# Four slots in thirteen summed, and 0.5 carried from the second layer's relu: a four-layer graph network on one core

## The chip, the cores and the metric

The kernel runs on one core of one Trainium2 chip. The metric is the device time of one launch in microseconds (us). Three runs of the kernel before gave 4869.19, 4869.73 and 4886.89 us; the median is 4869.73 us. All figures about where time goes come from one further, profiled execution, whose own time was 4870.96 us.

## The reference

The input is `x` with 64 graphs of 256 nodes and 128 features, and one 256 x 256 adjacency `adj`. Four layers follow each other, each of the form `h = relu(layernorm(x)); x = x + layer(h)`:

```
layer 0: five steps of a gated recurrent unit, fed by adj @ h
layer 1: relu([h, A h, (2 A A - 1) h, ...] @ Theta1 + bias)
layer 2: y = (adj @ h + h) @ weight + bias;  y / max(|y|, 1e-12)
layer 3: pre[i,j,:] = s1[i,:] + s2[j,:] + b_lin
         e[i,j] = sum_e a[e] * leaky_relu(pre[i,j,e]) + adj[i,j]
         sigmoid(softmax_j(e) @ h)
```

Layer 3 is the large one: for every graph, 256 x 256 pairs of nodes with 256 features each. The kernel computes the final sigmoid as `0.5 + 0.5 * tanh(...)`, and that 0.5 is one subject of the change. A layernorm subtracts the mean of a row, so a constant added to the whole row leaves what it returns as it was.

## The kernel before, in words

The graphs go in 32 pairs (`NPAIR`), two graphs at a time. For each pair a long chain of small steps, `front` (L484 on), computes layers 0 to 2 and the projections that layer 3 needs. The scores of layer 3 are then built in *slots*: 64 per pair, 2048 in all. A slot stands for four nodes of one 128-node half, one out of each group of 32, in both graphs, against all nodes and features. The features come in two halves of 128, and each half of a slot is a *tile* of 128 x 2048 float32 values: an elementwise minimum or relu of one projected value per partition against a row of the other projection. So there are 4096 tiles. `work_on_tile` (L910) makes them on whichever of three engines takes them: VectorE makes one with one instruction (L930), ScalarE with eight activations of 128 x 256 (L942), and GpSimd with eight tensor-scalar instructions of 128 x 256 (L947). Fourteen buffers (`rl`) hold tiles. TensorE reduces a tile over its partitions into a bank of PSUM with four matmuls of 32 columns (`score`, L1006), each recorded as two passes in float32.

In some slots the two halves are summed first, so that TensorE has one tile to reduce and not two. `JOINED` lists those slots from the constant `SHARE`: of the first 1952 slots (the last `ALONE` = 96 are left out) one in three, that is 650. For a joined slot, the sum is made by a DMA that GpSimd issues and that adds one buffer onto another (`add_pair`, L967). The buffer added from comes free when this DMA has landed; the other, when TensorE has read it.

The order of the work is made while the program is written. A planner keeps a clock per engine and hands out steps by modelled durations: `ran(DVE, 2.2, ...)` for a VectorE tile, 1.43 for half a ScalarE tile, 0.9 for a quarter of a GpSimd tile, `ISSUE` = 0.65 for the issue of a DMA, `LANDED` = 6.6 until it has landed, and named constants (`TURN`, `STATS` and others, L456 to L458) for the steps of a front. The engine whose clock stands lowest takes, of what is ready then, a step of a tail first, then of a front, and a tile only when no such step is ready. `in_order` then fixes that order: on the chip, each engine runs its own list strictly in that sequence and waits where something it needs is late. A changed modelled duration therefore changes no instruction, but it moves instructions in the lists and decides which engine makes which tile.

When the tiles of 32 slots have been reduced, `tail` (L805) finishes them on two banks' worth of rows: VectorE adds the odd feature's term (L812, two instructions from PSUM into PSUM) and the linear row (L816, from PSUM into SBUF), takes the row maximum (L821), ScalarE does the exponential (L825), TensorE turns and multiplies, ScalarE takes tanh (L849, two instructions), and VectorE makes `o = 0.5 * tanh + x3` (L853), which a DMA from SP's queue stores. The 0.5 of the sigmoid is in `x3` by then: GpSimd adds it in place (L713), once per pair, after the last layernorm has read `x3`.

Of the kernel before, what the change touches and what calls it, by code (L numbers as in the profile page):

```python
# [10 lines left out]
OP = mybir.AluOpType  # L11
# [3 lines left out]
P = 128  # L15
NB = 2
# [5 lines left out]
MOST_POSITIVE = -MOST_NEGATIVE  # L22
PE, DVE, ACT, POOL = ENGINES = (mybir.EngineType.PE, mybir.EngineType.DVE, mybir.EngineType.Activation, mybir.EngineType.Pool)
SLOTS = 64
SHARE = (1, 3)
AHEAD_OF = 2
ALONE = 96
LOW = 1
# [4 lines left out]
def kernel(  # L33
# [50 lines left out]
    nc = tc.nc  # L84
    B, N, D = x.shape
# [21 lines left out]
    def ran(engine, us, *after):  # L107
        start = max(clock[engine], 0.0, *after)
        if engine == ACT:
            behind[0] = max(0.0, behind[0] - (start - clock[ACT])) + 0.024 * us  # L110
        clock[engine] = start + us
        return clock[engine] + SEEN[engine] + (behind[0] if engine == ACT else 0.0)
# [13 lines left out]
    def by_feature(b, nb=NB):  # L126
        return b[:, 0:nb * N].rearrange("p (b n) -> p b n", b=nb)
# [64 lines left out]
    bias1 = load_row(l1_bias, "bias1")  # L192
# [71 lines left out]
    def other_constants():  # L264
# [5 lines left out]
        t = ran(DVE, 0.8)  # L270

        for c in range(NC):
            yield PE, t, 1
            b = take()
            for k in range(NC):
                nc.tensor.matmul(b[0][:, 0:N], adj_t[:, k, c * P:(c + 1) * P], adj_n[:, k, :], start=(k == 0), stop=(k == NC - 1))
            t = ran(PE, 1.2, t, b[1])
            yield DVE, t
            nc.vector.tensor_scalar(adj_2[:, c, :], b[0][:, 0:N], 2.0, None, op0=OP.mult)
            t = ran(DVE, 0.35, t)  # L280
# [1 line left out]
        yield DVE, 12.0  # L282
        nc.vector.tensor_add(th[:, 1:3, :], th_raw[:, 1:3, :], th_raw[:, 3:5, :])
        nc.vector.tensor_sub(th[:, 0, :], th_raw[:, 0, :], th[:, 2, :])
        ran(DVE, 0.5)
        yield DVE, clock[DVE]
        small = work.tile([P, 32], F32, name="small", bufs=1)

# [14 lines left out]
        t = ran(DVE, 1.5)  # L303
        yield PE, t, 1
        b = take()
# [5 lines left out]
        t = ran(PE, 0.6, t, b[1])  # L311
        yield DVE, t
        nc.vector.tensor_copy(columns(14, 3), b[0][:, 0:3])
        t = ran(DVE, 0.1, t)
# [27 lines left out]
        t = ran(DVE, 1.6)  # L342
# [11 lines left out]
        for c in range(NC):  # L354
            yield PE, t, 1
            b = take()
# [3 lines left out]
            t = ran(PE, 1.2, t, b[1])  # L360
# [5 lines left out]
            t = ran(DVE, 0.35, t)  # L366
# [3 lines left out]
        b = take()  # L370
# [8 lines left out]
        t = ran(PE, 1.4, t_in, b[1])  # L379
# [9 lines left out]
        t = ran(DVE, 0.9, t)  # L389
# [54 lines left out]
    def feat(name, **kw):  # L444
        return work.tile([P, NB, N], F32, name=name, **kw)
# [7 lines left out]
    SHORT = dict(tag="short", bufs=12)  # L453


    PROJECT, MIX, TURN, PRODUCT, PRODUCTS = (None, 0.44, 0.86), (None, 0.88, 1.74), (None, 0.55, 0.80), (None, 0.45, 0.88), (None, 1.33, 2.64)  # L456
    COPY, BIASED, TANH, ELEMENTS = (None, 0.32, 0.48), (None, 0.40, 0.58), (None, 0.40, 0.57), (None, 0.36, 0.61)
    NORMED, STATS, LAST = (None, 0.78, 1.55), (None, 0.40, 0.8), (None, 0.55, 1.04)  # L458

    def norm(src, since, h):  # L460

        nb = src.shape[1]
        stats = work.tile([P, nb * NC, 3], F32, name="stats", bufs=4)
        mv = work.tile([P, nb * NC, 2], F32, name="mv", bufs=4)
        s, h = rows_of(src), rows_of(h)[:, :, 0:D]
        yield DVE, since
        for k in range(0, nb * NC, 2):
            nc.vector.bn_stats(stats[:, k:k + 2, :].rearrange("p k s -> p (k s)"), s[:, k:k + 2, :].rearrange("p k d -> p d k"))
        nc.vector.tensor_reduce(mv[:, :, 0], stats[:, :, 1:2], AX.X, OP.add, negate=True)
        t = ran(DVE, STATS[nb], since) + 0.1  # L470
        yield POOL, t
        inverse_root(mv[:, :, 1], stats[:, :, 2], 1.0 / D, OP.mult, LN_EPS, OP.add)
        nc.gpsimd.tensor_mul(mv[:, :, 0], mv[:, :, 0], mv[:, :, 1])  # L473
        t = ran(POOL, 1.55, t)
        yield ACT, t
        for k in range(nb * NC):
            nc.scalar.activation(h[:, k, :], s[:, k, :], AF.Relu, bias=mv[:, k, 0:1], scale=mv[:, k, 1:2])  # L477
        return ran(ACT, NORMED[nb], t)
# [5 lines left out]
    def front(p, batches):  # L484
# [5 lines left out]
        alone = nb < NB  # L490
# [28 lines left out]
        def turned_of(b):  # L519
            return by_token(b[0], nb)  # L520
# [11 lines left out]
        t = yield from norm(x0, 20.0 if p else 3.0, h)  # L532
        yield PE, t, 1
        b = take()
        to_feature(b[0], h)
        t_h = t
        t = ran(PE, TURN[nb], t, b[1])
        yield ACT, t
        hT, t_hT = copied("hT", b, t, bufs=4)
        for step in range(STEPS):  # L540
            yield PE, t_h, 1, lambda: "adj" in SET_UP
            b = take()
            mix_nodes(b[0], h, adj_t)
            t = ran(PE, MIX[nb], t_h, b[1])
            yield ACT, t
            mT, t_m = copied("mT", b, t)
            if alone:
# [6 lines left out]
                t = ran(PE, PROJECT[nb], t_m)  # L554
# [6 lines left out]
            else:  # L561
# [4 lines left out]
                t = ran(PE, 2 * PROJECT[nb], t_m, t_hT, pr[1])  # L566
# [3 lines left out]
            t = ran(ACT, TANH[nb], t, r[1])  # L570
# [5 lines left out]
            if alone:  # L576
# [5 lines left out]
                t = ran(PE, PROJECT[nb], t_rh)  # L582
            else:
# [6 lines left out]
                t = ran(PE, 2 * PROJECT[nb], t_rh, pv[1])  # L590
# [6 lines left out]
            if alone:  # L597
                nc.scalar.activation(seen(pv), seen(pv), AF.Tanh, bias=bh, scale=1.0)
                t = ran(ACT, TANH[nb], t)
                yield DVE, t  # L600
                nc.vector.tensor_sub(d, seen(pv), hT)
                t = ran(DVE, ELEMENTS[nb], t)
                spare.append([pv[0], t])
            else:
                nc.scalar.activation(seen(pv), seen(pv), AF.Tanh, bias=bh_n, scale=-1.0)
                t = ran(ACT, TANH[nb], t)
                yield DVE, t
                nc.vector.tensor_add(d, seen(pv), hT)  # L608
                t = ran(DVE, ELEMENTS[nb], t)
# [3 lines left out]
            t = ran(DVE, ELEMENTS[nb], t, t_z)  # L613
# [7 lines left out]
            b = take()  # L621
            to_token(b[0], hT)
            t = ran(PE, TURN[nb], t_hT, b[1])
# [7 lines left out]
        x1 = token("x1", tag="x12", bufs=3)  # L631
        nc.vector.tensor_add(x1, x0, turned_of(b))
        t = ran(DVE, ELEMENTS[nb], t)
# [6 lines left out]
        b = take()  # L640
        mix_nodes(b[0], h, adj_n)
        t = ran(PE, MIX[nb], t_h, b[1])
# [3 lines left out]
        b = take()  # L646
        to_feature(b[0], h)
        t = ran(PE, TURN[nb], t_h, b[1])
        yield ACT, t
        hT, t = copied("hT", b, t, bufs=4)  # L650
        yield PE, t_h, 1
        b = take()
        mix_nodes(b[0], h, adj_2)
        t = ran(PE, MIX[nb], t_h, b[1])
        yield ACT, t
        c2T, t = copied("c2T", b, t)
        yield PE, t, 1
        po = take()
        project_token(po[0], [(hT, th[:, 0, :]), (c1T, th[:, 1, :]), (c2T, th[:, 2, :])])
        t = ran(PE, PRODUCTS[nb], t, po[1])  # L660
# [3 lines left out]
        t = ran(DVE, ELEMENTS[nb], t)  # L664
        yield DVE, t
        x2 = token("x2", tag="x12", bufs=3)
        nc.vector.scalar_tensor_tensor(x2, turned_of(po), 0.0, x1, op0=OP.max, op1=OP.add)
        t = ran(DVE, ELEMENTS[nb])
        spare.append([po[0], t])

# [2 lines left out]
        t = yield from norm(x2, t, h)  # L673
        yield PE, t, 1
        b = take()
        mix_nodes(b[0], h, adj_ti)
        t = ran(PE, MIX[nb], t, b[1])
        yield ACT, t
        yT, t = copied("yT", b, t)
        yield PE, t, 1  # L680
        po = take()
        project_token(po[0], [(yT, w2)])
        t = ran(PE, PRODUCT[nb], t, po[1])
# [3 lines left out]
        t = ran(DVE, ELEMENTS[nb], t)  # L687
# [21 lines left out]
        h3 = kept("h3", [NC, D + 1])  # L709
        nc.gpsimd.memset(h3[:, :, :, D:D + 1], 2.0)  # L710
        t = yield from norm(x3, t, h3)
        yield POOL, t
        nc.gpsimd.tensor_scalar(x3, x3, 0.5, None, op0=OP.add)  # L713
        ran(POOL, 0.45 if alone else 0.7, t)
        yield PE, t, 1
        b = take()
        to_feature(b[0], h3)
# [87 lines left out]
    def tail(u, pe, since):  # L805

        ops = READY[u]
        x3, h3, pe, lin = ops["x3"], ops["h3"], [by_feature(pe[0])[:, k, :] for k in range(NB)], ops["lin"]
        yield DVE, max(since, ops["t_lin"])
        sc = feat("sc", **SHORT)  # L810
        for k, (b, c) in enumerate(across(u)):
            nc.vector.scalar_tensor_tensor(pe[k], ops["s2o"][:, b, :], ops["s1o"][:, b, c:c + 1], pe[k], op0=OP.min, op1=OP.add)  # L812
        t = ran(DVE, 0.8, since, ops["t_lin"])
        yield DVE, t
        used = banks_of.pop(u)
        nc.vector.tensor_add(sc, by_feature(used), lin.to_broadcast([P, NB, N]) if ops["alone"] else lin)  # L816
        t = ran(DVE, ELEMENTS[2], t)
        spare.append([used, t])
        yield DVE, t
        nmx = work.tile([P, NB], F32, name="nmx")  # L820
        nc.vector.tensor_reduce(nmx, sc, AX.X, OP.max, negate=True)  # L821
        t = ran(DVE, ELEMENTS[2], t)
        yield ACT, t
        for b in range(NB):
            nc.scalar.activation(sc[:, b, :], sc[:, b, :], AF.Exp, bias=nmx[:, b:b + 1], scale=1.0)  # L825
        t_s = ran(ACT, 0.8, t)
        yield PE, t_s, 1
        b = take()
        to_token(b[0], sc)
        t = ran(PE, TURN[2], t_s, b[1])  # L830
        yield ACT, t
        wT = tok("wT", **SHORT)
        nc.scalar.copy(wT, by_token(b[0]))
        t = ran(ACT, COPY[2], t)
        spare.append([b[0], t])
        yield PE, t, 1
        bank = take()
        po = bank[0][:, :NB * (D + 1)].rearrange("p (b d) -> p b d", b=NB)
        for k, (b, _) in enumerate(across(u)):
            for c in range(NC):  # L840
                side_by_side(po[:, k, :], wT[:, k, c, :], h3[:, b, c, :], c == 0, c == NC - 1)
        t = ran(PE, PRODUCT[2], t, bank[1])
        yield DVE, t
        rs = work.tile([P, NB], F32, name="rs")
        nc.vector.reciprocal(rs, po[:, :, D])
        t = t_s = ran(DVE, 0.15, t)
        yield ACT, t
        for k in range(NB):
            nc.scalar.activation(po[:, k, 0:D], po[:, k, 0:D], AF.Tanh, scale=rs[:, k:k + 1])  # L849
        t = ran(ACT, 0.5, t, t_s)  # L850
        yield DVE, t
        o = work.tile([P, NB, D], F32, name="o")
        nc.vector.scalar_tensor_tensor(o, po[:, :, 0:D], 0.5, x3[:, 0] if ops["alone"] else x3[:, :, u[1], :], op0=OP.mult, op1=OP.add)  # L853
        t = ran(DVE, 0.36, t)
        spare.append([bank[0], t])
        p, k = u
        nc.sync.dma_start(out[p * NB + k].rearrange("(c p) d -> p c d", p=P) if ops["alone"] else
                          out[p * NB:(p + 1) * NB, k * P:(k + 1) * P, :].rearrange("b p d -> p b d"), o)
        TAILED.add(u)
# [269 lines left out]
```

## Time and profile before

| | |
|---|---|
| median of three runs | 4869.73 us |
| profiled execution, its own time | 4870.96 us |
| span of the profile | 4869.2 us |
| TensorE busy (records) | 4729.6 us |
| VectorE busy | 4666.6 us |
| ScalarE busy | 4630.5 us |
| GpSimd busy | 4693.2 us |
| share of time that the 16 DMA engines spent on the summing queue | 69.9% |
| mean granted TensorE clock | 0.997 |

The profile lists busy time by engine, then groups of equal instructions with their count, the busy time of the group (time in which at least one of its records was open), the mean length of one record, and the idle time of the engine directly ahead of them with what ended it. Records of matmuls and activations overlap, so a mean length times a count is more than the busy time; what one instruction takes of its engine is better read as the distance between starts in a dense stretch of the timeline. "PE" is TensorE, "DVE" VectorE, "ACT" ScalarE, "POOL" GpSimd. A line such as L967 is the line of the kernel that issued the instruction.

### The profile page before, as it was taken

How to read it: one execution, taken by the hardware profiler on the slowest of the kernel's cores; microseconds unless marked ns; L12 is line 12 of the kernel's file. 1: busy time of each engine (PE TensorE's matmuls, PEld its weight loads, DVE VectorE, ACT ScalarE, POOL GpSimd, SP SyncE). 2: the span in 40 equal slices, each digit the busy share in tenths (PEclk: the TensorE clock that was granted, in tenths of full speed). 3: DMA queues.
4: the chain of work that ended last, by engine and by line, in shares of the span. 5: the costliest groups of instructions: out<-in, count | busy, mean ns of one | idle time of the engine just before them, and what ended most of it. 6: DMA issues, size and time to landing. Idle time of an engine off the chain costs nothing.

```text
span 4869.2 us, 134117 instructions
## 1 busy us (share of the span) xinstructions
PE 4729.6 (97%) x52183; PEld 1750.1 (36%) x52183; DVE 4666.6 (96%) x3571; ACT 4630.5 (95%) x12119; POOL 4693.2 (96%) x9914
## 2 busy tenths in 40 slices
PE   9999999999999999999999999999999999999999
PEld 4333333333333333333333333333333333333333
DVE  6999999999999999999999999999999999999998
ACT  6999999999999999999999999999999999999999
POOL 3999999999999999999999999999999999999998
PEclk9999999999999999999999999999999999999999
DMA  1778777777777787777877777877777777787830
GB/s 46 158 148 165 159 155 160 158 153 163 156 158 156 149 165 160 153 162 152 165 160 155 160 153 156 166 156 155 163 147 162 161 160 157 154 163 155 165 65 5
DMA packets 138729, 725.21 MB, mean 149 GB/s; under 512 B 15721, under 2 KB 50921, under 8 KB 54889
## 3 DMA queue, kind: packets, MB, share of 16 engines
q0 software_dynamic: 93600, 681.62, 69.9%
q1 hardware_dynamic: 43768, 35.01, 2.5%
q8 instruction: 408, 6.68, 0.5%
q14 instruction: 233, 1.90, 0.1%
q10 hardware_dynamic: 720, 0.00, 0.0%
HBM read 26.48 MB, written 8.52 MB: 7 GB/s over the span
## 4 chain that ended last, share of the span: by engine, by line
PE 48%; POOL 16%; DVE 15%; DMA 10%; ACT 6%; issue 4%; POOLq 0%; DVEq 0%; SPq 0%; ACTq 0%
PE bank L1006 29%; PE bank L402 17%; POOL rl L947 13%; DVE rl L930 12%; DMA rl<-rl 10%; ACT rl L942 4%; POOL rl L967 1%; PE bank L433 1%; PE bank L425 1%; POOL mv L397 1%; DVE hT L616 1%; DVE bank L612 0%; ACT h L477 0%; DVE d L608 0%; DVE rh L573 0%
## 5 line engine op out<-in xcount | busy, mean ns | idle before, releaser
L930 DVE TENSOR_TENSOR rl<-s1a,bank 128x2048 f32<-128x2048 f32 x1751 | 3921.6, 2279 | 105.7 <-DMA rl<-rl 75.4
L942 ACT ACTIVATE rl<-bank,s1b 128x256 f32<-128x256 f32 x10032 | 3946.2, 691 | 75.4 <-DMA rl<-rl 48.1
L947 POOL TENSOR_SCALAR rl<-s2n,s1b 128x256 f32<-128x256 f32 x6352 | 3043.6, 789 | 28.4 <-DMA rl<-rl 8.6
L1006 PE MATMUL bank<-rl,win_n 128*32 128x512 f32 x17536 | 2209.3, 594 | 49.0 <-DMA rl<-rl 46.3
L1006 PE MATMUL bank<-rl,win 128*32 128x512 f32 x10032 | 1331.7, 594 | 0.0
L947 POOL TENSOR_SCALAR rl<-s2c,s1a 128x256 f32<-128x256 f32 x2376 | 1155.4, 747 | 5.0 <-DMA rl<-rl 0.7
L1006 PEld LDWEIGHTS bank<-rl,win_n 128*32 128x32 f32 x17536 | 568.9, 110 | 1195.5 <-issue 929.9
L967 POOL DMA_DIRECT2D rl<-rl x650 | 689.4, 1077 | 9.4 <-PE bank L1006 2.2
L1006 PEld LDWEIGHTS bank<-rl,win 128*32 128x32 f32 x10032 | 330.3, 110 | 637.1 <-issue 525.3
L402 PE MATMUL bank<-mT,wts 128*32 128x512 f32 x2480 | 324.9, 592 | 0.2 <-ACT mT L525 0.2
L402 PE MATMUL bank<-adj_t,h 128*32 128x256 f32 x4960 | 299.0, 380 | 7.8 <-ACT h L627 7.6
L402 PEld LDWEIGHTS bank<-adj_t,h 128*32 128x32 f32 x4960 | 160.3, 110 | 170.0 <-issue 42.8
L477 ACT ACTIVATE h<-x,mv 128x128 f32<-128x128 f32 x376 | 162.7, 572 | 41.3 <-POOL mv L473 41.2
L402 PE MATMUL bank<-rh,u5t 128*32 128x512 f32 x1240 | 162.1, 593 | 8.0 <-DVE rh L573 7.9
L402 PE MATMUL bank<-hT,wts 128*32 128x512 f32 x1240 | 164.1, 596 | 0.0
L402 PE MATMUL bank<-mT,w 128*32 128x512 f32 x1240 | 162.4, 593 | 0.4 <-ACT bank L569 0.4
L569 ACT ACTIVATE bank<-bank,gate_b 128x512 f32<-128x512 f32 (+1 forms) x165 | 138.5, 840 | 20.9 <-PE bank L402 13.6
L402 PEld LDWEIGHTS bank<-mT,wts 128*32 128x32 f32 x2480 | 81.6, 110 | 186.0 <-issue 149.6
L397 POOL TENSOR_TENSOR mv<-mv,minus_half 128x4 f32<-128x4 f32 (+1 forms) x132 | 134.0, 1015 | 11.0
L525 ACT COPY mT<-bank 128x512 f32<-128x512 f32 x155 | 119.5, 771 | 26.2 <-PE bank L402 26.0
L592 ACT ACTIVATE bank<-bank,gate_b 128x512 f32<-128x512 f32 (+1 forms) x165 | 134.1, 813 | 10.2 <-PE bank L402 9.9
L433 PE MATMUL bank<-ident,hT 128*128 128x128 f32 x620 | 101.5, 286 | 38.1 <-DVE hT L616 37.8
(206 smaller groups left out, 3354.9 us busy)
## 6 DMA issues: line engine op xcount, KB each, us to landing
rl<-rl POOLq DMA_DIRECT2D x650, 1024.0 KB, 8.4
rows<-row SPq DMA_DIRECT2D x31, 512.0 KB
xin<-in_x_dram SPq DMA_DIRECT2D x64, 128.0 KB
out_dram<-o SPq DMA_DIRECT2D x64, 128.0 KB
row<-quarter SPq DMA_DIRECT2D x62, 2.0 KB
rows<-row SPq DMA_DIRECT2D x2, 256.0 KB
w_raw<-in_L_gnn_w_w_dram SPq DMA_DIRECT2D x3, 128.0 KB
rl<-in_L_gnn_Theta_dram SPq DMA_DIRECT2D x1, 320.0 KB
```

The lines of the kernel that those rows point to most:

```text
L397: nc.gpsimd.tensor_tensor(t, t, minus_half[:, 0:t.shape[1]], op=OP.pow)
L402: nc.tensor.matmul(o[g:g + 32], w[:, g:g + 32], t, start=start, stop=stop, skip_group_check=True)
L433: nc.tensor.transpose(pt[:, b, c, :], ht[:, b, c * P:(c + 1) * P], ident)
L477: nc.scalar.activation(h[:, k, :], s[:, k, :], AF.Relu, bias=mv[:, k, 0:1], scale=mv[:, k, 1:2])
L525: nc.scalar.copy(c, seen(bank))
L569: nc.scalar.activation(seen(r), seen(pr), AF.Tanh, bias=br, scale=0.5)
L592: nc.scalar.activation(seen(pr), seen(pr), AF.Tanh, bias=bz, scale=0.5)
L930: nc.vector.tensor_tensor(t, rows.to_broadcast(whole), ops["s2a"].unsqueeze(1).to_broadcast(whole), op=OP.min)
L942: nc.scalar.activation(t[:, g, b, :], other(ops["s2p"][0], b), AF.Relu, bias=rows[:, g, b], scale=-1.0)
L947: nc.gpsimd.tensor_scalar(t[:, part, b, :], other(ops["s2n" if k else "s2c"], b), rows[:, part, b], MOST_NEGATIVE, op0=OP.min, op1=OP.max)
L967: nc.gpsimd.dma_start(out=t.rearrange("p g b n -> p (g b n)"), in_=z.rearrange("p g b n -> p (g b n)"), accum_op=OP.add)
L1006: nc.tensor.matmul(pe[g * 32:(g + 1) * 32, :], w[:, 31 - r:63 - r], flat(t[:, g]), start=False, stop=(left[u] == 0), skip_group_check=True)
```

## The change

The final 0.5 is no longer added to `x3`. Layer 1's output is `x2 = x1 + relu(p + bias)`. The layernorms of layers 2 and 3 take the constant out again, and `x3` inherits it. The GpSimd instruction of each pair is deleted.

In the tail, the linear row is added first, in place in PSUM, and the odd feature's term second, from PSUM into SBUF: the same three VectorE instructions with other destinations.

`SHARE` goes from one slot in three to four in thirteen: 600 joined slots, not 650. Five modelled durations of the planner change: `TURN` from 0.55 and 0.80 to 0.38 and 0.60, `STATS` from 0.40 and 0.80 to 0.50 and 0.87, the GpSimd part of a norm from 1.55 to 1.69, and the tanh of a tail from 0.5 to 0.9. They are no instructions, but the planner lays out every list anew with them.

```
-SHARE = (1, 3)
+SHARE = (4, 13)
...
+        nc.vector.tensor_scalar(bias1, bias1, 0.5, None, op0=OP.add)
+        ran(DVE, 0.7)
...
-    ..., TURN, ... = ..., (None, 0.55, 0.80), ...
+    ..., TURN, ... = ..., (None, 0.38, 0.60), ...
-    NORMED, STATS, LAST = (None, 0.78, 1.55), (None, 0.40, 0.8), (None, 0.55, 1.04)
+    NORMED, STATS, LAST = (None, 0.78, 1.55), (None, 0.50, 0.87), (None, 0.55, 1.04)
...
-        t = ran(POOL, 1.55, t)
+        t = ran(POOL, 1.69, t)
...
-        nc.vector.scalar_tensor_tensor(x2, turned_of(po), 0.0, x1, op0=OP.max, op1=OP.add)
+        nc.vector.scalar_tensor_tensor(x2, turned_of(po), 0.5, x1, op0=OP.max, op1=OP.add)
...
-        yield POOL, t
-        nc.gpsimd.tensor_scalar(x3, x3, 0.5, None, op0=OP.add)
-        ran(POOL, 0.45 if alone else 0.7, t)
...
+        used = banks_of.pop(u)
+        nc.vector.tensor_add(by_feature(used), by_feature(used), lin.to_broadcast([P, NB, N]) if ops["alone"] else lin)
+        t = ran(DVE, ELEMENTS[2], since, ops["t_lin"])
+        yield DVE, t
         sc = feat("sc", **SHORT)
         for k, (b, c) in enumerate(across(u)):
-            nc.vector.scalar_tensor_tensor(pe[k], ops["s2o"][:, b, :], ops["s1o"][:, b, c:c + 1], pe[k], op0=OP.min, op1=OP.add)
+            nc.vector.scalar_tensor_tensor(sc[:, k, :], ops["s2o"][:, b, :], ops["s1o"][:, b, c:c + 1], pe[k], op0=OP.min, op1=OP.add)
-        t = ran(DVE, 0.8, since, ops["t_lin"])
-        yield DVE, t
-        used = banks_of.pop(u)
-        nc.vector.tensor_add(sc, by_feature(used), lin.to_broadcast([P, NB, N]) if ops["alone"] else lin)
-        t = ran(DVE, ELEMENTS[2], t)
+        t = ran(DVE, 0.8, t)
...
-        t = ran(ACT, 0.5, t, t_s)
+        t = ran(ACT, 0.9, t, t_s)
```

More of the change, by code (lines that the diff above doesn't have):

```diff
@@ L284, in other_constants @@
         nc.vector.tensor_sub(th[:, 0, :], th_raw[:, 0, :], th[:, 2, :])
-        ran(DVE, 0.5)
+        nc.vector.tensor_scalar(bias1, bias1, 0.5, None, op0=OP.add)
+        ran(DVE, 0.7)
         yield DVE, clock[DVE]
@@ L453 @@
     SHORT = dict(tag="short", bufs=12)
-    PROJECT, MIX, TURN, PRODUCT, PRODUCTS = (None, 0.44, 0.86), (None, 0.88, 1.74), (None, 0.55, 0.80), (None, 0.45, 0.88), (None, 1.33, 2.64)
+    PROJECT, MIX, TURN, PRODUCT, PRODUCTS = (None, 0.44, 0.86), (None, 0.88, 1.74), (None, 0.38, 0.60), (None, 0.45, 0.88), (None, 1.33, 2.64)
     COPY, BIASED, TANH, ELEMENTS = (None, 0.32, 0.48), (None, 0.40, 0.58), (None, 0.40, 0.57), (None, 0.36, 0.61)
-    NORMED, STATS, LAST = (None, 0.78, 1.55), (None, 0.40, 0.8), (None, 0.55, 1.04)
+    NORMED, STATS, LAST = (None, 0.78, 1.55), (None, 0.50, 0.87), (None, 0.55, 1.04)
     def norm(src, since, h):
```

## The prediction

> **What bounds the kernel now.** I read the page's busy line first, then the groups, the chain that ended last, the waits, and the timeline for real distances between starts.
>
> ```profile
> span 4869.2 us, 134117 instructions
> PE 4729.6 (97%) x52183; PEld 1750.1 (36%) x52183; DVE 4666.6 (96%) x3571; ACT 4630.5 (95%) x12119; POOL 4693.2 (96%) x9914
> PE 48%; POOL 16%; DVE 15%; DMA 10%; ACT 6%; issue 4%; POOLq 0%; DVEq 0%; SPq 0%; ACTq 0%
> ```
>
> Four engines are within 2% of each other, and the chain (third line) runs over all of them, with summing DMAs as a tenth of it. No engine alone sets the end. The stretches say when:
>
> ```profile
> 0.00:92.00 92.00, 83.61 (x1185) 44.62 (x1189) 46.97 (x145) 46.46 (x109) 14.81 (x43) 1.00 0.10 28
> 92.00:4740.00 4648.00, 4524.94 (x49901) 1656.59 (x49905) 4504.26 (x3363) 4465.53 (x11689) 4567.36 (x9625) 1.00 0.76 155
> 4740.00:4850.00 110.00, 110.00 (x1012) 44.22 (x1012) 108.83 (x58) 109.39 (x303) 110.00 (x246) 1.00 0.02 4
> ```
>
> The columns after the length are busy PE, PEld, DVE, ACT, POOL, then clock, DMA share and GB/s. The first 92 us are set-up and the first front, which the change barely touches. From there to 4740 us POOL is busy 98.3%, DVE 96.9%, ACT 96.1%. PE's 97.4% is too high: in the timeline
>
> ```profile
> 1000.58 1.04 PE L1006 MATMUL bank<-rl,win 128*32 128x512 f32 x8
> 1001.44 1.90 PE L1006 MATMUL bank<-rl,win_n 128*32 128x512 f32 x16
> 1003.15 1.04 PE L1006 MATMUL bank<-rl,win 128*32 128x512 f32 x8
> ```
>
> a tile's eight records are open for 1.04 us but the next tile starts 0.86 us later, so every run of matmuls hides up to 0.18 us of possible waiting. Counting by such distances (3446 tiles x 0.86 = 2964; a front 5 x (one mix 1.73 + five projections of 0.86 + one turn 0.58) = 33 and about 14 for its layers 1 to 3, so 47 x 32 = 1504; 64 tails at 2.35 = 150) PE works about 4620 us, some 95% of the span. POOL works nearest its limit; PE has more air than its busy line says.
>
> ```profile
> L947 POOL TENSOR_SCALAR rl<-s2n,s1b 128x256 f32<-128x256 f32 x6352 | 3043.6, 789 | 28.4 <-DMA rl<-rl 8.6 <-ACT s1b L782 5.1 <-DVE x L667 1.8
> L967 POOL DMA_DIRECT2D rl<-rl x650 | 689.4, 1077 | 9.4 <-PE bank L1006 2.2 <-issue 2.2 <-POOL rl L947 2.1
> L713 POOL TENSOR_SCALAR x<-x 128x512 f32<-128x512 f32 (+1 forms) x33 | 48.4, 1468 | 3.8 <-ACT h L477 1.3
> L812 DVE SCALAR_TENSOR_TENSOR bank<-rows,s1o,bank 128x256 f32<-128x256 f32 x128 | 62.4, 487 | 16.8 <-PE bank L1006 14.1 <-issue 0.3
> L816 DVE TENSOR_TENSOR sc<-bank,rows 128x512 f32<-128x512 f32 x64 | 43.7, 682 | 0.0
> ```
>
> These are the groups that the change touches. The waits on the summing DMA:
>
> ```profile
> DVE rl L930 <- DMA rl<-rl: 75.4, 60, 3.8
> ACT rl L942 <- DMA rl<-rl: 48.1, 28, 4.4
> PE bank L1006 <- DMA rl<-rl: 46.3, 41, 2.8
> ```
>
> DVE and ACT wait for a buffer that a DMA still reads, PE for a sum not yet landed: 170 us over three engines, the largest waits that cross engines in the joined stretch.
>
> **What the skill says.** The Trainium skill, "Perfetto Trace Analysis", Identifying the Most-Contended Engine: matmul busy time is no fair measure of TensorE's headroom, while occupancy is for the others. The trace agrees (1.04 us open against 0.86 us apart). "DMA: Bandwidth & Descriptors", SWDGE vs HWDGE vs iDMA: accumulating DMAs must be issued by GpSimd, whose cores compute the descriptors, so a join costs POOL time; the trace agrees (row L967). "VectorE: DVE Perf Modes", The perf-mode tier table: a float32 operand in PSUM holds `tensor_tensor` to one element a cycle. The trace agrees: L816 into SBUF takes 682 ns, and L663, the same operation into PSUM, 694 ns.
>
> **The change part by part.** Counts come from the instruction lists of the two built programs.
>
> *Joins.* 50 DMA issues go. A record lasts 1.08 us, but in the timeline an issue at 2421.69 is followed by the next GpSimd tile at 2422.32, so it takes 0.63 us: 50 x 0.63 = 31.5 us off POOL. In return PE reduces 3496 tiles, not 3446: 50 x 0.86 = 43 us onto PE.
>
> *The 0.5.* L713 is deleted: 48.4 us off POOL (1.51 us each; in the timeline the next tile starts 1.58 us after it). Nobody waits for it, so its worth is POOL's time alone. The constant in L667 costs nothing more; the one `bias1` instruction lies in the set-up, below 0.3 us by L816's size. It adds a wait for the load of `bias1`, with the first fronts' VectorE steps behind it; that load follows `theta`'s on SP's queue, for which the two instructions ahead of it wait anyway, so 0 to 2 us, and I take 0.
>
> *Tiles.* POOL gets 11 tiles more (1102), ACT 7 fewer (1247), DVE 4 fewer (1747). A POOL tile takes 3.60 us (2418.14 to the next work at 2421.69): +39.6. A DVE tile takes 2.24 (3921.6 / 1751): -9.0. An ACT tile takes 2.97 (16 activations in 5.93 us are two tiles): -20.8.
>
> *The tail's order.* The add goes PSUM to PSUM (694 ns in L663's row against 682), the odd term PSUM to SBUF; L616 against L612 is the same pair of destinations, 679 against 692. Per tail 0.69 + 2 x 0.48 against 0.97 + 0.68: within 0.02 us, 1 us in all. The length to the maximum, and when the bank comes free, are unchanged; both orders wait for the same row DMA. SP's list has 243 instructions in both; no transfer but the 50 joins goes.
>
> *The modelled durations.* No instruction, but new lists. By the trace, the old ones had L713 at 0.7 (is 1.5: 31 x 0.8 = 25 us that the plan did not know of on POOL), the tail's tanh at 0.5 (two records of 0.51 in a row, 64 x 0.4 = 26 us on ACT), and a turn at 0.80 (four transposes take 0.6: 312 x 0.2 = 62 us that PE didn't need). The new list's lateness against its plan should be less. It can't be read off the trace; I bound it by -15 and +15 us and take -4, a tenth of ACT's 48.5 us of waiting for a norm's POOL part.
>
> *Sum by engine:* POOL -31.5 - 48.4 + 39.6 = -40; ACT -21; DVE -9; PE +43.
>
> POOL, DVE and ACT draw on one stock of tiles. Weighted by their shares of the chain (16, 15, 6): (16 x 40 + 15 x 9 + 6 x 21) / 37 = 24 us shorter. Their waits for the DMA are 133 us with POOL's 9.3, or 44 each. One join in thirteen fewer takes 3 us of it by count; the queue, busy 69.9%, clears faster, so up to a fifth (9 us): I take 7. PE's 43 us must come out of some 240 us in which it is not working, about 90 of which are at the two ends: at 4840 us it would work about 97% of the middle. I take 5 us lost on the way, where a bank or buffer is released later; the ends are 0 (all in the gaps) and 43.
>
> Sum: -24 - 7 + 5 - 4 = -30 us against the profiled 4871 us (span 4869.2 and 1.8 around it), which is 1.2 us above the median: about 4840 us.
>
> **Rivals.**
>
> *It cancels.* Take the chain's shares at face value for all four. PE holds 48%, so its 43 us cost 0.48 x 43 = 21. POOL gives 0.16 x 40 = 6.4, DVE 1.4, ACT 1.3. The chain's DMA share is 502 us; 50 of 650 fewer would be 39, but a route only a few us shorter takes the place of each, so a fifth, 8, stays. Net +4: about 4874 us. For it: the long PE pieces in the chain. Against it: PE is fed by the three others, and a PE piece on the chain may be one that merely ran while they would have been next.
>
> *TensorE becomes the bound, slower.* In 4740 to 4850 us, where nothing is joined, PE is busy without a gap: fewer joins move the middle towards that. PE's waits on the front (38 us for turned hidden states, about 35 for other steps) don't shrink, and if POOL's relief only fills buffers sooner, the whole 43 us less some 9 of DMA waiting is added: 4903 us; half-way, 4887. It decides once PE's real share in the middle goes over about 98%; I reckon 97%. Against it: POOL is at 98.3% with PE at 95 to 96%.
>
> *The re-made plan is much better*, beyond 15 us: less lateness on all engines, 4790 us. Nothing in the profile prices it.
>
> That the change doesn't do what it says is excluded by the lists: 600 joins, no L713.
>
> **How the numbers follow.** First case (relief of the elementwise engines) 0.62, own range 4815 to 4862; cancels 0.20; PE the bound 0.15; better plan 0.03. 0.5% is 24 us, about what a measurement of this kernel can tell from no change: below 4845 is faster, above 4894 slower. The first case gives 0.44 faster and 0.18 same; the second 0.02, 0.15 and 0.03; the third 0.03 same and 0.12 slower; the last 0.03 faster. Together 0.49, 0.36, 0.15. The range 4805 to 4892 holds the first case with the bounds of the plan's lateness, the second, and half-way to the third.
>
> **What would show it.** Right: 600 issues at L967; POOL's busy time down by about 40 us, PE's records up by about 45; the DVE and ACT waits for DMA down from 75 and 48; POOL's share of the chain down and PE's up. A PE busy over 98.5% with longer DVE and ACT waits on L1006 (13.8 and 19.5 us now) would show the slower rival. Wrong also if the DMA waits grow in spite of fewer joins, which only the new order could do.

## The result, and the profile after

The kernel after takes 4796.69 us (median of four runs, 4794.88 to 4801.95) against 4869.47 us for the kernel before measured with it. (One of the four runs of before took 4886.89 us; the other three lie within 0.6 us of each other.) The ratio is 0.984, with a 95% interval of 0.982 to 0.987: 73 us, or about 1.5%, faster. The forecast was 4840 us, with a range from 4805 to 4892, and faster at a chance of 0.49. So the sign was right, the forecast gain of 30 us was less than half of what came, and the time lies below the range.

The head of the profile of the kernel after: span, busy time by engine, and the chain that ended last.

```profile
span 4794.6 us, 134766 instructions
PE 4744.3 (99%) x52583; PEld 1758.2 (37%) x52583; DVE 4651.6 (97%) x3568; ACT 4608.6 (96%) x12063; POOL 4636.5 (97%) x9919
PE 69%; DVE 10%; POOL 8%; DMA 6%; ACT 5%; issue 2%; POOLq 0%; SPq 0%; DVEq 0%; ACTq 0%
```

PE now has a record open during all but 50 us of the span (140 before), and it holds 69% of the chain (48% before). Three engines have less work and one has more. The span is down by 75 us, and busy time by 15 us on DVE, 22 on ACT and 57 on POOL. For DVE and ACT the larger part of the 75 us is therefore waiting that is gone; for POOL it is work. Two rows of before, whose idle time matters:

```profile
L930 DVE TENSOR_TENSOR rl<-s1a,bank 128x2048 f32<-128x2048 f32 x1751 | 3921.6, 2279 | 105.7 <-DMA rl<-rl 75.4
L942 ACT ACTIVATE rl<-bank,s1b 128x256 f32<-128x256 f32 x10032 | 3946.2, 691 | 75.4 <-DMA rl<-rl 48.1
```

The same two after, with the groups that the prediction named:

```profile
L940 ACT ACTIVATE rl<-bank,s1b 128x256 f32<-128x256 f32 x9976 | 3937.4, 704 | 47.5 <-DMA rl<-rl 18.7
L928 DVE TENSOR_TENSOR rl<-s1a,bank 128x2048 f32<-128x2048 f32 x1747 | 3909.3, 2276 | 41.4 <-DMA rl<-rl 19.5
L945 POOL TENSOR_SCALAR rl<-s2n,s1b 128x256 f32<-128x256 f32 x6408 | 3056.0, 799 | 19.5 <-ACT s1b L780 5.1
L1004 PE MATMUL bank<-rl,win_n 128*32 128x512 f32 x17992 | 2241.6, 593 | 20.8 <-DMA rl<-rl 14.9
L965 POOL DMA_DIRECT2D rl<-rl x600 | 644.9, 1090 | 3.6 <-PE bank L1004 0.9
```

(L928, L940, L945, L965, L1004 are L930, L942, L947, L967 and L1006 of before.) 600 issues stand where 650 stood, L713 is gone, and the waits for the summing DMA are 19.5 us on DVE, 18.7 on ACT and 14.9 on PE, where they were 75.4, 48.1 and 46.3. Idle time ahead of DVE's tiles fell from 105.7 to 41.4 us. Yet a sum took hardly less time to land. These are the issues of the sums, before and after, and their last number is the median time in us from issue to landing:

```profile
rl<-rl POOLq DMA_DIRECT2D x650, 1024.0 KB, 8.4
rl<-rl POOLq DMA_DIRECT2D x600, 1024.0 KB, 8.3
```

In the stretch from 92 to 4665 us, PE has a record open 99.3% of the time (97.4% in the middle before), and POOL is busy 98.7%:

```profile
92.00:4665.00 4573.00, 4539.28 (x50276) 1669.61 (x50272) 4488.19 (x3355) 4444.16 (x11635) 4514.78 (x9638) 1.00 0.72 146
```

### The profile page after: what moved, and what is told of

Read it like the earlier page. It is cut to its first block, busy times and chain, and to the rows that moved or that the text cites. A ratio compares the mean times of both kernels' runs of the same rounds, so it can differ in the third digit from the quotient of the medians.

```text
span 4794.6 us, 134766 instructions
## 1 busy us (share of the span) xinstructions
PE 4744.3 (99%) x52583; PEld 1758.2 (37%) x52583; DVE 4651.6 (97%) x3568; ACT 4608.6 (96%) x12063; POOL 4636.5 (97%) x9919
## 4 chain that ended last, share of the span: by engine, by line
PE 69%; DVE 10%; POOL 8%; DMA 6%; ACT 5%; issue 2%; POOLq 0%; SPq 0%; DVEq 0%; ACTq 0%
PE bank L1004 43%; PE bank L403 23%; DVE rl L928 8%; POOL rl L945 7%; DMA rl<-rl 5%; ACT rl L940 3%; PE bank L434 2%; PE bank L426 1%; POOL rl L965 1%; ACT h L478 0%; DVE bank L613 0%; DVE d L609 0%; DVE hT L617 0%; DVE rh L574 0%; POOL mv L398 0%
## 5 line engine op out<-in xcount | busy, mean ns | idle before, releaser
L940 ACT ACTIVATE rl<-bank,s1b 128x256 f32<-128x256 f32 x9976 | 3937.4, 704 | 47.5 <-DMA rl<-rl 18.7
L928 DVE TENSOR_TENSOR rl<-s1a,bank 128x2048 f32<-128x2048 f32 x1747 | 3909.3, 2276 | 41.4 <-DMA rl<-rl 19.5
L945 POOL TENSOR_SCALAR rl<-s2n,s1b 128x256 f32<-128x256 f32 x6408 | 3056.0, 799 | 19.5 <-ACT s1b L780 5.1
L1004 PE MATMUL bank<-rl,win_n 128*32 128x512 f32 x17992 | 2241.6, 593 | 20.8 <-DMA rl<-rl 14.9
L1004 PE MATMUL bank<-rl,win 128*32 128x512 f32 x9976 | 1317.3, 593 | 0.0
L945 POOL TENSOR_SCALAR rl<-s2c,s1a 128x256 f32<-128x256 f32 x2408 | 1167.1, 763 | 3.5
L1004 PEld LDWEIGHTS bank<-rl,win_n 128*32 128x32 f32 x17992 | 577.4, 110 | 1197.8 <-issue 978.2
L965 POOL DMA_DIRECT2D rl<-rl x600 | 644.9, 1090 | 3.6 <-PE bank L1004 0.9
L1004 PEld LDWEIGHTS bank<-rl,win 128*32 128x32 f32 x9976 | 324.8, 110 | 636.4 <-issue 516.5
L606 ACT ACTIVATE bank<-bank,gate_b 128x512 f32<-128x512 f32 x155 | 128.8, 831 | 6.3 <-PE bank L403 6.3
```

The costliest lines, as they stand in the source:

```text
L928: nc.vector.tensor_tensor(t, rows.to_broadcast(whole), ops["s2a"].unsqueeze(1).to_broadcast(whole), op=OP.min)
L940: nc.scalar.activation(t[:, g, b, :], other(ops["s2p"][0], b), AF.Relu, bias=rows[:, g, b], scale=-1.0)
L945: nc.gpsimd.tensor_scalar(t[:, part, b, :], other(ops["s2n" if k else "s2c"], b), rows[:, part, b], MOST_NEGATIVE, op0=OP.min, op1=OP.max)
L965: nc.gpsimd.dma_start(out=t.rearrange("p g b n -> p (g b n)"), in_=z.rearrange("p g b n -> p (g b n)"), accum_op=OP.add)
L1004: nc.tensor.matmul(pe[g * 32:(g + 1) * 32, :], w[:, 31 - r:63 - r], flat(t[:, g]), start=False, stop=(left[u] == 0), skip_group_check=True)
```

## The experiments

The change has four parts: the *share* (600 joins), the *modelled durations* (four steps, not five: the turn, the statistics, the norm's GpSimd part and the tanh), *L713* deleted, and the *tail's order*. The expectations weigh five theories of where the 73 us come from:

- L: fewer joins alone clear the DMA queue.
- P: the corrected durations make the planned order fit the chip.
- W: it is the work taken off GpSimd, chiefly L713.
- I, formed after the first four experiments: share and turn need each other.
- C: the order that comes out is luck.

### Each part alone, and all without the share

```
e1_share          before:  SHARE = (1, 3)  ->  (4, 13)
e2_model          before:  TURN, STATS, the norm's 1.55 and the tanh's 0.5  ->  those of after
e3_half           before:  bias1 + 0.5, max with 0.5 in x2, L713 deleted
e4_after_third    after:   SHARE = (4, 13)  ->  (1, 3)
```

> The kernel before with SHARE (4, 13) alone: 600 joins, 3496 tiles to reduce; lists give DVE 1760, ACT 1232, POOL 1104 tiles. Theory L (fewer summing DMAs clear the queue, and that is where the waits went): most of the 73 us, 4800 to 4825, with the DVE and ACT waits for the summing DMA falling from 75 and 48 to below 30 each. Theory P (the corrected modelled durations make the order fit the chip): only the work counts, POOL -31 + 13 x 3.6 = +15 us, DVE +20, ACT -65, PE +43: 4860 to 4880, waits for the DMA lower by a tenth at most. Theory W (work taken off POOL, chiefly the deleted addition): 4860 to 4875.

> The kernel before with the four modelled durations of after (turn, statistics, norm, tanh) and nothing else: the same instructions in another order. Theory P: most of the gain, 4800 to 4830, and PE's idle time before the turns (38 us) falls. Theory L and W: no instruction goes, 4855 to 4880, DMA waits as before.

> The kernel before with the 0.5 carried from layer 1's relu: L713 gone, 48 us less on POOL, 8 tiles more for it. Theory W: 4835 to 4850, POOL's relief shared over three engines (48 / 3 = 16) and the lateness that the plan did not know of gone as well. Theories L and P: 4850 to 4865.

> The kernel after with SHARE back at one in three, all else kept: 650 joins. Theory L: most of the gain is lost, 4840 to 4860, DMA waits of DVE and ACT together above 90 us. Theory P: most is kept, 4795 to 4815. Theory W: half, 4825 to 4845.

| | us | ratio to before, 95% |
|---|---|---|
| e1_share | 4887.8 | 1.0036 (1.0023 to 1.0049) |
| e2_model | 4893.9 | 1.0049 (1.0034 to 1.0064) |
| e3_half | 4853.9 | 0.9967 (0.9952 to 0.9981) |
| e4_after_third | 4852.2 | 0.9966 (0.9953 to 0.9979) |

Neither the share nor the durations alone gain anything, both are slower; deleting L713 gains 15 us. The three add up to 28 us slower, yet together they are 73 us faster. Theories L and P fall as stated. (e4_after_third lies in L's range, but the waits of DVE and ACT for the sums are 60 us there and not above 90.) So does W: 15 us are less than its 19 to 34, and in the range of L and P. The share is worth 55 us on top of the rest, and costs 18 us without it. Theory I was formed from this.

The waits for the summing DMA show two different troubles. On PE in e1_share (600 joins, old durations):

```profile
PE bank L1006 <- DMA rl<-rl: 6.1, 8, 2.6
```

On PE in e2_model (650 joins, new durations), and in e4_after_third, which differs from after in the share alone:

```profile
PE bank L1006 <- DMA rl<-rl: 76.4, 78, 3.5
PE bank L1004 <- DMA rl<-rl: 67.0, 59, 3.5
```

On ACT in e1_share:

```profile
ACT rl L942 <- DMA rl<-rl: 108.6, 47, 7.0
```

With 600 joins and the old durations, PE hardly ever waits for a sum (6 us), but ACT waits 109 us for a buffer that a sum still reads. With the corrected durations and 650 joins, ACT waits less for buffers (35 us), but PE stands 76 us in front of sums that haven't landed. In after both are small, 14.9 on PE and 18.7 on ACT.

### Which duration, and how much is luck

```
e9_after_oldturn     after:   TURN = (None, 0.38, 0.60)  ->  (None, 0.55, 0.80)
e10_after_onlyturn   after:   STATS 0.50, 0.87 -> 0.40, 0.8;  norm 1.69 -> 1.55;  tanh 0.9 -> 0.5
e6_nudge_b           before:  ELEMENTS = (None, 0.36, 0.61)  ->  (None, 0.36, 0.62)
e7_nudge_a           after:   the same
```

> The kernel after with TURN alone back at 0.55 and 0.80: 600 joins, no L713, other modelled durations corrected. Theory I (the plan charged PE 62 us too much, which it could bear with 650 joins but not with 600, so that its order holds tiles back on the chip too): most of the gain is lost, 4855 to 4885, ScalarE makes 19 tiles fewer than in after and waits for buffers; DVE and ACT waits for the DMA above 100 us together. Theory C (which order comes out is luck, and any change of a modelled duration moves the time by some 20 us either way): anything from 4800 to 4880, no more likely high than low. Theory L (joins alone): 4795 to 4815.

> The kernel after with the statistics, the norm and the tanh back at their old modelled durations, TURN corrected. Theory I: the gain stays, 4790 to 4810, PE idle below 70 us. Theory C: 4790 to 4870. If the tanh's 26 us of lateness on ACT matters: 4815 to 4830.

> The kernel before with one modelled duration moved by a hundredth of a us (ELEMENTS of a pair 0.61 to 0.62), which changes the order and no instruction's work. It measures how much an order of this kind varies by chance. Theory C: off by 15 us or more from 4869. Theories I and L: within 10 us of it.

> The kernel after with the same hundredth of a us. Theory C: 4815 or more, the good order was a lucky one. Theories I and L: within 10 us of 4797.

e9_after_oldturn took 4844.9 us (ratio 0.9949, 0.9934 to 0.9964), e10_after_onlyturn 4807.0 (0.9873, 0.9857 to 0.9890). So of the four durations it is the turn that matters, by 48 us against 10 for the other three, which is within what an order varies by (below). Theory I's range, 4855 to 4885, was too high by ten at its lower end; its direction and its sign in the lists hold: the group of ACT's tiles in e9_after_oldturn is

```profile
L940 ACT ACTIVATE rl<-bank,s1b 128x256 f32<-128x256 f32 x9824 | 3861.2, 678 | 110.0 <-DMA rl<-rl 60.0 <-PE bank L1004 31.6 <-POOL rl L945 10.0
```

9824 activations are 1228 tiles, 19 fewer than in after, and ACT idles 110 us ahead of them instead of 47.5.

The nudges change no work, only the order. They moved the kernel before to 4889 and 4909 us in two runs, 30 us up, and the kernel after to 4812 (0.9882), 15 us up; that lies between what I and L foresaw (within 10 us) and what C did (4815 or more). Theory C is right to this extent: one order among its like is worth some 15 us either way, and a comparison of two kernels whose lists are re-planned carries that uncertainty however well it is timed. It is not right on the gain: after and its nudged twin are 57 us or more below before and its twin.

### What GpSimd's time is worth, and where PE binds

```
e14_after_l713   after:   the 0.5 back in L713 (planned at 0.7), out of bias1 and x2
e15_dummy        after, behind the last norm of each pair, with no entry in the plan:
                 + nc.gpsimd.tensor_tensor(spin[:, 0], spin[:, 0], spin[:, 1], op=OP.pow)
e13_quarter      after:   SHARE = (4, 13)  ->  (7, 25)
e8_priced        before:  L713's ran(POOL, 0.45 if alone else 0.7, t)  ->  0.9 if alone else 1.5
```

> The kernel after with the 0.5 back where it was, as L713 in the plan at 0.7, and the constant out of layer 1: so the kernel before with the share, the modelled durations and the tail's order changed. If L713 costs its own POOL time shared over three engines (48 / 3 = 16 us): 4805 to 4820. If what it costs is its whole POOL time or more (POOL, or the lateness it brings, passes on to all): 4835 to 4855. Theory I (share and turn together carry the gain) holds in both; it falls if this is above 4860.

> The kernel after with one more GpSimd instruction in each pair at the place where the last norm ends, a power of six numbers of a small tile of its own that nobody reads: about 1.5 us each (four numbers take 1.03 us now), 33 times, and every other instruction in exactly the order of after. It prices unplanned work on GpSimd alone. Shared over three engines can't be, since the lists are fixed: if POOL's time passes on in full, +40 to +55 us (4840 to 4850); if PE is the bound now (its records are busy 99%) and POOL has slack, +0 to +20 (4797 to 4815).

> The kernel after with SHARE (7, 25): 546 joins, 54 fewer still, so PE reduces 3550 tiles (+46 us) and POOL issues 34 us less, with 17 tiles more. If PE is the bound of the kernel after (rival of the prediction): 4825 to 4845, PE without idle time. If fewer joins still help because the waits for the DMA go: 4775 to 4795.

> The kernel before with L713 kept but told to the plan at its measured length (1.5 for 0.7 us, 0.9 for 0.45). If the cost of L713 is the lateness that the plan did not know of: 4845 to 4860. If it is the work: 4865 to 4885, and chance of the order, +-20 us, on top of both.

e15_dummy took 4834.1 us (0.9927, 0.9913 to 0.9942). The added group reads

```profile
L715 POOL TENSOR_TENSOR spin<-spin 128x6 f32<-128x6 f32 x33 | 44.8, 1359 | 0.0
```

VectorE, ScalarE and GpSimd run the rest in exactly the order of after, so no chance of re-planning enters: 44.8 us of unplanned GpSimd time cost 37.4 us, 0.83 of it. (The single instruction took 1.36 us and not the 1.5 expected, and the cost was a little below the +40 to +55 foreseen for it.) GpSimd's time is not shared with the engines that make the other tiles, because the lists are fixed when the plan is made. The time turns up elsewhere, as waits for sums, which GpSimd issues:

```profile
DVE rl L931 <- DMA rl<-rl: 56.6, 49, 3.2
ACT rl L943 <- DMA rl<-rl: 43.7, 33, 4.0
PE bank L1007 <- DMA rl<-rl: 29.6, 40, 2.3
```

These are 130 us where after has 53, with the same 600 sums in the same order and a median landing time of 8.2 us. So neither the number of sums nor their landing time settles how long engines wait for them; here a late GpSimd did. e14_after_l713 took 4858.0 us (0.9976, 0.9967 to 0.9984), 61 above after and just over the range for "its whole time or more"; a second order, below, gives 4849.

e8_priced took 4846.8 (0.9954, 0.9939 to 0.9969): the instruction stays, the plan merely knows how long it is, and 23 us are gone, more than the 15 that deleting it brought in e3_half. Two such orders can't be ranked to 10 us, but the work need not go for a gain of this size to come. (L713 kept but correctly priced was not run with the share and the other durations of after.)

e13_quarter took 4829.2 (0.9917, 0.9901 to 0.9934), 33 above after. Its chain:

```profile
PE 75%; DVE 9%; POOL 6%; DMA 4%; ACT 3%; issue 2%; POOLq 0%; DVEq 0%; ACTq 0%
```

With 54 joins fewer PE has 54 x 0.86 = 46 us more to do, and the time is longer by 0.70 of that. This fits the rival that PE becomes the bound. But it is one order of one share; where between 650 and 546 joins the limit lies was not measured.

### Second orders of the same kernels, the tail, the landing time

```
n_third            e4_after_third,   ELEMENTS 0.61 -> 0.62
n_oldturn          e9_after_oldturn, ELEMENTS 0.61 -> 0.62
n_l713             e14_after_l713,   ELEMENTS 0.61 -> 0.62
n_before2          before,           MIX = (None, 0.88, 1.74)  ->  (None, 0.88, 1.75)
e16_oldtail        after:   odd term PSUM to PSUM first, then the linear row PSUM to SBUF
e12_after_landed   after:   LANDED 6.6  ->  8.0
```

> The kernel after with SHARE one in three (as e4_after_third, 4852 us), nudged by the hundredth of a us in ELEMENTS. Mechanism (650 summing DMAs hold up a plan that is otherwise right): 4835 to 4870. Chance: it may fall to 4800 to 4820.

> The kernel after with the old TURN (as e9_after_oldturn, 4845 us), nudged by the same hundredth. Mechanism (the plan's overcharged PE holds tiles back from ScalarE, 1232 tiles here): 4830 to 4865. Chance: 4800 to 4820.

> The kernel before with another nudge, MIX of a pair 1.74 to 1.75. With e6_nudge_b (4899) and before itself (4869) it says where the kernel before stands among its like: if 4880 to 4905, its own order was a good one and the change's typical gain is above 73 us; if 4850 to 4870, the first nudge was an unlucky one.

> The kernel after with the tail's three VectorE instructions in the old order (odd term in PSUM first, linear row second). The prediction's step says 0: 4790 to 4815, which is the chance of the order around after and its twin. If the new order of the tail matters in itself, 4820 or more.

> The kernel after with L713 back (as e14_after_l713, 4858 us), nudged by the hundredth of a us in ELEMENTS. If L713 costs what fixed-order work costs (0.85 of its time, 41 us, on a typical after of 4805): 4835 to 4860, so 4858 was on the high side. If it costs 60: 4855 to 4880.

> The kernel after with LANDED, the plan's time from a summing DMA's issue to its landing, at 8.0 and not 6.6 us (measured median 8.3). The same instructions, DVE 1748, ACT 1247, POOL 1101 tiles. If the remaining waits for sums (15 us on PE, 38 on DVE and ACT) are the plan's short landing time: 4770 to 4790. If buffers are the limit, so that a later planned release only holds tiles back: 4800 to 4825.

The planner has a forecast of its own: where the latest of its engines' clocks stands when the last step has been handed out. It follows from each kernel's source alone and is no measurement. It counts from after the set-up, so only differences between rows mean anything. The measured time less this forecast is called lateness here.

| kernels of one kind (joins, turn, L713) | orders, us | mean | planner's forecast, mean | lateness |
|---|---|---|---|---|
| before's kind (650, old, kept) | 4869, 4899, 4879 | 4882 | 4747 | 135 |
| after's kind (600, new, deleted) | 4797, 4812, 4807, 4796, 4792 | 4801 | 4732 | 69 |
| 650 joins, else after | 4852, 4872 | 4862 | 4774 | 88 |
| old turn, else after | 4845, 4856 | 4850 | 4787 | 63 |
| L713 kept, else after | 4858, 4849 | 4854 | 4747 | 107 |
| share alone (e1_share) | 4888 | 4888 | 4784 | 104 |
| durations alone (e2_model) | 4894 | 4894 | 4765 | 129 |
| L713 deleted alone (e3_half) | 4854 | 4854 | 4747 | 107 |

n_third was 4872.1 us (1.0007, 0.9998 to 1.0016), n_oldturn 4855.6 (0.9973, 0.9964 to 0.9983), n_before2 4878.5 (1.0021, 1.0013 to 1.0029), n_l713 4849.2 (0.9962, 0.9947 to 0.9978). n_third is 2 us above the range that it was given for the mechanism, and n_before2 between its two ranges. Every kernel that lacks one of the three parts lies at 4844.9 or above in every order run, and every kernel with all three, nothing added and 600 joins, at 4812 or below. So the joint gain is no accident of one order. Taken from the means, leaving out the share loses 61 us, the turn 49, L713 53. Adding them alone to before's kind makes it 5 (e1_share) and 11 us slower (e2_model, all four durations; the turn alone was not run on before) and 29 faster (e3_half), each from a single order. Before's own order was the best of its three; its kind is 81 us above after's.

The last two columns say where these losses arise. The turn's is all in the forecast (55 us): with 600 joins and the old turn, the planner believes PE to have 4751 us of work in a plan of 4787, and with the corrected one 4686 in after's 4729. L713's is mostly lateness (38 of 53), and the share's is in both (42 and 19). Alone, the share makes the plan longer by 37 us, since PE's added work goes onto a PE that the plan takes to be full. This is the part of "share and turn need each other" that the plan shows.

e16_oldtail took 4796.4 (0.9852, 0.9836 to 0.9869), which is after to 0.3 us: the tail's order is worth nothing. (Its planner's forecast is after's to the digit, so after's kind has four orders of its own, not five.) e12_after_landed took 4792.2 (0.9842, 0.9826 to 0.9859); DVE's wait for the DMA fell from 19.5 to 11.1 us,

```profile
DVE rl L928 <- DMA rl<-rl: 11.1, 19, 1.8
```

and all four engines' waits for sums fell from 57 to 20 us. Its 4.5 us against after lie between the two ranges foreseen and within what an order varies by, and its interval overlaps after's. It is the fastest measured, not shown to be better; 37 us less of these waits did not shorten the time by as much.

## Why the prediction was right or wrong

**The counts and the prices of single instructions** held: 600 issues, L713 gone, PE's work up by 50 tiles, nothing for the tail's order (e16_oldtail). POOL's busy time was to fall by about 40 and fell by 57. PE's records were to rise by 45 and rose by 15. By the prediction's distances between starts PE has 3496 x 0.86 + 1504 + 150 = 4661 us of work, 97% of the span of 4794.6. If that count is right, the waiting that runs of matmuls hide (up to 0.18 us each) has shrunk; this was not measured.

**The step that failed: "The new list's lateness against its plan should be less ... I bound it by -15 and +15 us and take -4".** The forecast has -24 us for the work moved, and -7, +5 and -4, together -6, for what else runs late or early. The planner's forecast fell by 15 us (4743.5 to 4728.9), so the first term was not far off. Lateness fell by 58 us, from 126 to 68 (by 66 between the means of the kinds). That is nearly four times the bound. The prediction said that this can't be read off the trace. That there was much to gain could be seen by setting the planner's clock beside the measured time of the kernel before; how much of it would go could not.

Part of it had been named and then lost. L713 was half unplanned: 0.7 of its 1.5 us was in the plan, and 31 x 0.8 = 25 us was not. The prediction worked out these 25 us and then put the lateness at 4 us for all durations together. At the price that e15_dummy found, 0.83, they alone are 21 us, and e8_priced, which corrects the plan and leaves the work, gained 23. In the table L713 is worth 38 us of lateness with the rest of the change, and 28 without it. What makes up the difference to 21 stays open; the order's chance is of that size.

**"POOL, DVE and ACT draw on one stock of tiles", weighted by their shares of the chain,** holds for work that the plan knows. It gave L713's whole 48.4 us a weight of 16 in 37, which is 21 us. On the chip, engines can't share what comes late, and deleting L713 was worth 29 to 53 us.

**The turn's "62 us that PE didn't need" was put aside,** and by the table it is worth 49 us with 600 joins. In the plan it is the room for 50 more tiles on PE. With the old turn ACT is given 1228 and 1232 tiles rather than 1247, and waits for buffers.

**The step "the queue, busy 69.9%, clears faster, so up to a fifth (9 us): I take 7" had the cause wrong as well as the size.** DVE, ACT and POOL waited 133 us for the summing DMA before and 42 after, 30 us each on average, while the median landing time went from 8.4 to 8.3 us. With the share alone (e1_share) the same waits are 186 us, and in e15_dummy 101. That leaves when the lists issue the sums and free the buffers; this was not measured directly.

**PE's 43 us, "I take 5".** With the old turn they arrive nearly in full in the plan (37 us, share alone); with the corrected one, the planner's forecast with 600 joins is the shorter. e13_quarter shows 0.70 of such time arriving in the measured time, once PE is at 99%. A reading behind this term is not borne out by the records: of 140 us in which PE has no record open before, 8 lie in the first 92 us and 9 in the last 20,

```profile
4850.00:4870.00 20.00, 11.09 (x98) 4.70 (x90) 6.55 (x8) 9.10 (x24) 1.04 (x3) 0.76 0.03 7
```

and not "about 90". With 90 there, the prediction's own numbers leave under 80 us of idle time in a middle of some 4730 us. PE would be working about 98% of it, where the rival "TensorE becomes the bound" was to decide, and not 97%.

That rival was wrong for this change; e13_quarter agrees with it for the next 54 joins. The rival "it cancels" took each engine's share of the chain as its price. In e15_dummy GpSimd's time has a price of 0.83, although POOL holds 8% of the chain of after. "The re-made plan is much better", 4790 us at a chance of 0.03, was nearest the measured time, and its mechanism, "less lateness on all engines", is what the runs show for 58 of the 73 us. As it said, nothing in the profile prices it.

## What to carry to other kernels

Where engines run lists fixed in advance, price an edit against the plan and not only against the engine: work that the plan knows is shared out, work that it doesn't know passes on nearly in full (0.83 here), and a modelled duration that is too long takes away room that the next edit needs. Set the plan's own forecast beside the measured time first: here 126 us, the set-up included, lay between them before and 68 after. Where four engines are within 2% of each other, test edits together before dropping one that does nothing alone. And run a second order of the same work (a duration moved by a hundredth) before believing any difference of 15 us between two planned kernels.

## What the runs showed that was not expected

A hundredth of a us in one modelled duration moved the time by 30 us (0.6%) with the same work; the planner's forecast moved by 5 us only. Runs of one order agree within 0.1 to 0.2% for most kernels; that nudged order's two runs are 20 us apart, but both lie above every run of the kernel before beside them.

On GpSimd, after the in-place addition over 128 x 512 the next instruction starts 1.58 us later, where eight instructions over 128 x 256 take 3.60 us together, 0.45 each: more than three times as long for twice the elements. No run says why. A power of six numbers per partition has a record of 1.36 us and one of four 1.02, so the longer of these costs as much as three instructions over 256 elements.
